# Three small broadcasts in a four-layer convolution network: from TensorE products to a round trip through memory

## The chip, the cores and the metric

The kernel runs on one core of a Trainium2 chip, in float32 throughout. The metric is the device time of one execution in microseconds. A core has TensorE (PE, with its weight loads listed apart as PEld), VectorE (DVE), ScalarE (ACT), GpSimd (POOL) and SyncE (SP), which here only issues DMAs. Each engine works through its own instructions in order.

## The reference

The input is x of shape (8, 384, 32, 32). Four layers follow one another; each adds f(GroupNorm(x)) to x. Layer 0 is an attention with depthwise convolutions ahead of it. The change concerns layers 1 and 3, and their order beside layer 2.

```
# layer 1: mixture of 4 experts, two of them kept for each token (h, w)
scores = softmax(x_flat @ gate_w + gate_b);  top_v, top_i = top_k(scores, 2)
top_w  = softmax(top_v)                       # two weights a token, their sum is 1
coef[e] = sum over k of present[k, e] * top_w[k]
out = sum over e of (w2[e] @ relu(w1[e] @ x + b1[e]) + b2[e]) * coef[e]

# layer 2: depthwise 3x3 with ternary weights, then a pointwise product

# layer 3: deformable attention, 3 groups of 128 channels
q   = q_w @ x
off = gelu(batchnorm(depthwise 5x5, stride 2, of q))         # 16 x 16 points a group
om  = pw_w @ off                                             # 3 rows: y, x, modulation
offset, modulation = om[0:2], sigmoid(om[2:3])
pos = tanh(offset) * (1/16) * 2 + reference points
x_s = bilinear samples of x at pos, times sigmoid(modulation)
k, v = kv_w @ x_s;  out = proj_w @ attention(q, k, v) + proj_b
```

## The kernel before, in words

Channels lie on the 128 partitions, in KC = 3 chunks; an image has N = 1024 pixels, and HALF is 512. Layer 0 takes the first half of the time and is not touched. What follows is one pass over the eight images.

**Layer 1** of an image is a list of 48 units (`layer1`, from L1184). For each half of the pixels there are 12 hidden units (`hidden`, L1260: three matmuls of 128 x 512, a Relu on ScalarE, and in `weight` a product with the token's coefficient on VectorE, L1246), and then 12 result units (`result`, L1281: three matmuls each; four units make one 128-channel output, which VectorE adds to x at L1287). `enter` forms the unit's input. In between stand two small steps for each half:

- `spread(h)` (L1219 to L1228) brings the tokens' first weight w0 to all partitions. `route` leaves w0 as [128 tokens, 8 images x 8 blocks]. Four matmuls (L1224) take a column of it, repeated 128 times, as the stationary operand and the identity as the moving one; VectorE copies the PSUM bank into the tile w0s (L1228), which has one buffer.
- `bias(h)` (L1233) and `weight` (L1242, on ScalarE) read w0s.

The first image is run in another way (`late=True`): its hidden units are done while the routing is still open.

**Layers 2 and 3** of an image are generators. Layer 2 takes statistics (L103), normalises (L144), does the nine taps on VectorE (L1347, L1355), then the pointwise product (`pw`, L1363), and stores x through SP (L1371). Layer 3 makes q (L1400), transposes the image into xT (L1423), does 25 taps for the offsets on VectorE (L1470) and a Gelu (L1475). Then it makes `om`: for each of three rows r, the weights of the row, repeated over 128 columns (`pw3[:, r, :]`), are multiplied with the 768 points in two matmuls (L1483, L1484), so that the row's result stands on all 128 partitions; ScalarE's Tanh (L1487) brings it from PSUM into the tile om{r}. From gy and gx (rows 0 and 1; L1493, L1497) come "tents", relu(1 - |position - pixel|), on ScalarE (L1501, L1502, L1515, L1516), multiplied on GpSimd (L1517); from row 2 comes md (L1498, L1499). Eight blocks of pixels are sampled by matmuls of xT with the tents (L1521, tiles xsb and xs), and VectorE multiplies with md (L1528). Keys and values (L1535, L1544), the attention (L1561 to L1614) and the last product (`pf`, L1666) follow.

**The order.** In the main loop image b's layers 2 and 3 run beside image b+1's layer 1. The generator yields numbers, the microseconds in which TensorE is held to have nothing of this image to do; they are added up in `due`, and whenever `due` reaches UNIT = 2.6, one unit of layer 1 is issued. What is left of the 48 units is issued after the generator has ended. The yields of one image are:

| part of the image | yields, us |
|---|---|
| layer 2 up to the end of the taps | 43.3 |
| layer 3 up to the Gelu and the break (`yield None`) | 44.85 |
| the three om rows | 3 x 0.3 |
| the elementwise work on om | 6.0 |
| the first sampled block's tents; the eight blocks | 2.0; 8 x 0.5 |
| up to the end of the attention | 17.5 |

At b = 6 the remaining units are all issued at the break; what follows of image 6 runs beside image 7's layers 2 and 3. When the program is built, an instruction may be put ahead of others of its engine that are not ready: in the trace the next image's entry (L1211) runs ahead of this image's last product. The tiles of tag "flat" (five buffers of 4 KB a partition) are shared by loads of layer 0's output, the offsets, the tents and the attention's probabilities. PSUM has two tiles of two banks ("big"), three banks for layer 1 (`fbank`) and one more (`vbank`).

**Queues.** Almost all DMAs are issued by SP, in order: the stores of x after layer 2 (L1371), the next image's loads (`load_image` L169, which waits for xT's buffer, and L1195, which waits for flat buffers), and the output (L1677).

```
offf = off.rearrange("p g h w -> p (g h w)")
nc.scalar.activation(offf, offf, AF.Gelu, bias=bo3, scale=so3)
yield 3.0
yield None
...
while due >= UNIT and units:
    units.pop(0)()
    due -= UNIT
```

Of the kernel before, what the change touches and what calls it, by code (L numbers as in the profile page):

```python
# [7 lines left out]
F32 = mybir.dt.float32  # L8
AF = mybir.ActivationFunctionType
# [3 lines left out]
B, C, H, W = 8, 384, 32, 32  # L13
N = H * W
P = 128
KC = C // P
HALF = N // 2
# [15 lines left out]
NPAIR3, HS, LS, NG = 3, 16, 256, 3  # L33
# [19 lines left out]
def tile_kernel(ctx: ExitStack, tc: tile.TileContext, i: dict, out: bass.AP):  # L53
    nc = tc.nc
# [4 lines left out]
    dram = ctx.enter_context(tc.tile_pool(name="dram", bufs=1, space=bass.MemoryType.DRAM))  # L59
# [157 lines left out]
    with ExitStack() as pa:  # L217
# [10 lines left out]
        for s in range(2):  # L228
            t = wa.tile([P, KC, H + 2, W], F32, name=f"pad{s}")
# [124 lines left out]
        with tc.issue_after(stacked[0].ins):  # L354
            load_x(1)
            nc.sync.dma_start(out=cw[:, 3:], in_=i["cw"][:, 3:])
            ident = load_const("ident")
# [6 lines left out]
        for n, (b, g) in enumerate(work):  # L364
# [6 lines left out]
            if n in todo:  # L371
                f, b2 = todo.pop(n)
# [10 lines left out]
            for h, k in steps:  # L383
                dx, c0, c1, o0 = TAPS[k]
                rows = slice(h * (H // 2), (h + 1) * (H // 2))
                if g < NGC:
                    lhs, rhs = cw[:, g, dx, :], st[:, rows, c0:c1]
                else:
                    r = slice(32 * h, 32 * h + 3 * GR)
# [550 lines left out]
    def load_w(name):  # L940
        src = i[name]
        t = wd.tile(list(src.shape), F32, tag=name, name=name + "_sb")
        nc.sync.dma_start(out=t, in_=src)
        return t
# [8 lines left out]
    def fbank(name):  # L953
        return ps_f.tile([P, HALF], F32, tag="f", name=name)
# [17 lines left out]
    pl = Pools(pd, "d")  # L972
    w1, b1 = load_w("w1"), load_w("b1")
    w0 = wd.tile([P, B, NT8], F32, name="w0")
    pres = wd.tile([P, 2, NE], F32, name="pres")
    nc.vector.memset(pres, 0.0)
    gws = wd.tile([P, NE], F32, name="gws")
# [58 lines left out]
    def route(units, end):  # L1036


        ls = pl.one([P, HALF], "ts", "ls")
        nc.vector.tensor_copy(ls, plog)  # L1040

        pt = fbank("plt").rearrange("p (q a b e) -> p q a b e", q=8, a=2, b=B)
        for q in range(4):
            nc.tensor.matmul(
                pt[:, q].rearrange("p a b e -> p (a b e)"), lhsT=ls[:, q * P : (q + 1) * P],
                rhs=sel2, start=True, stop=True,
            )
        nc.tensor.matmul(
            pt[:, 4, 0].rearrange("p b e -> p (b e)"), lhsT=ones,
            rhs=tb.rearrange("p b e -> p (b e)"), start=True, stop=True,  # L1050
        )
        gb = wd.tile([P, B, NE], F32, name="gb")
        nc.vector.tensor_tensor(
            gb, pt[:, 4, 0], gbias.unsqueeze(1).to_broadcast([P, B, NE]), ALU.add
        )
        nt = B * NT8
        lg = pl.one([P, B, NT8, NE], "vt", "lg")
        for a in range(2):
            for q in range(4):
                nc.vector.tensor_tensor(lg[:, :, 4 * a + q, :], pt[:, q, a], gb, ALU.add)  # L1060
        l = lg.rearrange("p b t e -> p (b t) e")
        wk = pl.one([P, 3, nt, NE], "kt", "routing")
        wv = pl.one([P, 5, nt], "om2", "routed")

        def bc(ap):
            return ap.unsqueeze(2).to_broadcast([P, nt, NE])

        sc, eq, oh = (wk[:, k] for k in range(3))
        m = wv[:, 4]
        nc.vector.reduce_max(m, l, AX.X)  # L1070
        nc.vector.tensor_tensor(l, l, bc(m), ALU.subtract)
        nc.scalar.activation(sc, l, AF.Exp)
        nc.vector.reduce_sum(m, sc, AX.X)
        nc.vector.reciprocal(m, m)
        nc.vector.tensor_tensor(sc, sc, bc(m), ALU.mult)
        tops = []
        for k in range(2):
            mk, ek = wv[:, 2 * k], wv[:, 2 * k + 1]
            nc.vector.reduce_max(mk, sc, AX.X)

            nc.vector.tensor_tensor(eq, sc, bc(mk), ALU.is_equal)
            nc.vector.tensor_tensor(
                eq, eq, ewt.unsqueeze(1).to_broadcast([P, nt, NE]), ALU.mult
            )
            nc.vector.reduce_max(ek, eq, AX.X)
            nc.vector.tensor_tensor(oh, eq, bc(ek), ALU.is_equal)
            nc.vector.reduce_max(pres[:, k, :], oh.rearrange("p t e -> p e t"), AX.X)
            if k == 0:
                nc.vector.scalar_tensor_tensor(sc, oh, -2.0, sc, ALU.mult, ALU.add)
            tops.append(mk)  # L1090
        while len(units) > end:
            units.pop(0)()
        pp_ = fbank("ppres")
        nc.tensor.matmul(
            pp_[:, : 2 * NE], lhsT=ones, rhs=pres.rearrange("p k e -> p (k e)"),
            start=True, stop=True,
        )
        nc.vector.tensor_scalar(
            prs.rearrange("p k e -> p (k e)"), pp_[:, : 2 * NE], 0.0, None, ALU.is_gt
        )  # L1100
        nc.vector.tensor_tensor(m, tops[1], tops[0], ALU.subtract)
        nc.scalar.activation(m, m, AF.Exp)
        nc.vector.tensor_scalar(m, m, 1.0, None, ALU.add)
        nc.vector.reciprocal(w0.rearrange("p b t -> p (b t)"), m)

    prs = wd.tile([P, 2, NE], F32, name="prs")
    dp = wd.tile([P, NE], F32, name="dp")
# [55 lines left out]


    x2_dram = dram.tile([B, P, KC, N], F32, name="x2")
    NU3 = 2 * NPAIR3
    rec3 = wd.tile([P, B * NU3, 16], F32, name="rec3")
    bad3 = wd.tile([P, 1], mybir.dt.int32, name="bad3")
# [15 lines left out]
    def layer1(pl, b, late=False):  # L1184
# [33 lines left out]

        def spread(h):  # L1219

            pw = fbank(f"w0_{b}_{h}")
            for t in range(4):
                wt = w0[:, b, 4 * h + t : 4 * h + t + 1].to_broadcast([P, P])
                nc.tensor.matmul(  # L1224
                    pw[:, t * P : (t + 1) * P], lhsT=wt, rhs=ident, start=True, stop=True
                )
            state["w0", h] = pl.one([P, HALF], "w0", f"w0s{b}_{h}")
            nc.vector.tensor_copy(state["w0", h], pw)  # L1228
# [64 lines left out]
        def unit(*calls):  # L1293
            units.append(lambda: [f(*a) for f, *a in calls])

        if late:
            for h in range(2):
                unit((enter, h), (hidden, h, 0))
                for k in range(1, NE * KC):
                    unit((hidden, h, k))  # L1300
            for h in range(2):
                for m in range(KC):
                    for part in range(4):

                        w, n = (0, part) if h == m == 0 else (1, 4 * m + part - 4)
                        first = []
                        if n == 0:
                            first += [(spread, w), (bias, w)]
                        if h == 0 and n < 4:
                            first += [(weight, w, 3 * n + k) for k in range(3)]  # L1310
                        unit(*first, (result, h, m, part))
            return units
        for h in range(2):
            if h == 0:
                unit((enter, 0), (spread, 0), (bias, 0), (hidden, 0, 0))
            else:
                unit((bias, 1), (hidden, 1, 0))
            for k in range(1, NE * KC):
                unit((hidden, h, k))
            for m in range(KC):  # L1320
                for part in range(4):
                    if h == 0 and m == 2 and part == 0:
                        unit((result, h, m, part), (enter, 1), (spread, 1))
                    else:
                        unit((result, h, m, part))
# [48 lines left out]
    def layer3(pl, b, xt, put, general):  # L1374
# [103 lines left out]
        yield None  # L1478

        om = []  # L1480
        for r in range(3):
            po = big(f"pom_{b}_{r}")
            nc.tensor.matmul(po[:, :512], lhsT=pw3[:, r, :], rhs=offf[:, :512], start=True, stop=True)  # L1483
            nc.tensor.matmul(po[:, 512:768], lhsT=pw3[:, r, :], rhs=offf[:, 512:], start=True, stop=True)  # L1484
            t = pl.one([P, NG * LS], f"om{r}", f"om{r}_{b}")

            nc.scalar.activation(t, po[:, : NG * LS], AF.Tanh, scale=1.0 if r < 2 else 0.5)  # L1487
            om.append(t)
            yield 0.3
# [195 lines left out]
    for b in range(1, B):  # L1685
        logits(b)
        del fetched[b, 0]
        for n in (2, 3) if b == 1 else (b + 2,):
            if n < B:
                fetch_next(n)  # L1690
        if b + 3 == B:
            w2, b2 = load_w("w2"), load_w("b2")
            wq3, wk3, wv3, wp3 = (load_w(n) for n in ("wq3", "wk3", "wv3", "wp3"))
            pb3, dw3, bn3, pw3 = (load_w(n) for n in ("pb3", "dw3", "bn3", "pw3"))
            ref3, npos = load_w("ref3"), load_w("npos")
        if b + 1 < B:
            for _ in range(3 if b < 6 else 2):
                units.pop(0)()
# [81 lines left out]
def _layouts(a):  # L1780
# [3 lines left out]
    L = {}  # L1784
# [49 lines left out]
    for n in "qk":  # L1834
# [27 lines left out]
    L["bn3"] = np.stack(  # L1862
        [a[f"L3_conv_{n}"] for n in ("dw_b", "bn_w", "bn_b", "bn_mean", "bn_var")], axis=1
    )
    L["pw3"] = np.repeat(a["L3_conv_pw_w"].T[:, :, None], P, axis=2)
    lin = np.linspace(0.5, HS - 0.5, HS, dtype=f) / f(HS) * f(2.0) - f(1.0)
    ref = np.stack([np.repeat(lin, HS), np.tile(lin, HS)])
# [26 lines left out]
```

## Time and profile before

| what | value |
|---|---|
| median of 3 runs | 3751.69 us (3746.74 to 3756.45) |
| the profiled execution | 3751.05 us, its span 3749.3 us |
| mean granted TensorE clock | 0.981 |
| HBM read, written | 122.64 MB, 75.50 MB |
| layer 1's result and hidden matmuls (L1281, L1260) | 490.2 and 483.3 us of PE |
| layer 2's taps (L1355) | 234.0 us of DVE |
| layer 3's taps (L1470) | 213.1 us of DVE |

A float32 matmul stands in the trace as two records; "x6" is three matmuls. In a timeline a row gives start, duration, engine, line, operation, written tile <- read tiles, sizes and count, and in brackets the idle time ahead of it with what ended it. In the waits view a row gives who waited for whom, the total, the number of times, and the longest.

### The profile page before, as it was taken

The numbers are of one execution on the slowest core, as the hardware profiler recorded it, in microseconds if no ns is written. First come the engines' busy times: TensorE is split into PE (matmuls) and PEld (weight loads), VectorE is DVE, ScalarE is ACT, GpSimd is POOL, SyncE is SP. The second block draws the span as 40 slices with busy tenths as digits, with TensorE's granted clock in tenths as the row PEclk, the third lists the DMA queues.
The fourth block names the chain that finished last, engine by engine and source line by source line (L and its number), as shares of the span: only waits on it lengthen the run. The fifth ranks groups of instructions, "written<-read, shape, count | busy, mean of one in ns | idle before, by whom it ended". The sixth has DMA issues, their size and how long they took to land.

```text
span 3749.3 us, 39325 instructions
## 1 busy us (share of the span) xinstructions
PE 3632.0 (97%) x15746; PEld 1533.0 (41%) x15746; DVE 1820.6 (49%) x2840; ACT 1280.2 (34%) x1536; POOL 199.5 (5%) x162
## 2 busy tenths in 40 slices
PE   7999999999999999999799999999999999999888
PEld 3444333333333333333244534444444444544433
DVE  6776223232323232333346557465663656547664
ACT  2222354545444454534112321323222232322222
POOL 0000100000000000000000010201001010010111
PEclk8999999999999999999899999999999999999898
DMA  6776311121212121211430000100001001010000
GB/s 198 232 251 229 131 54 36 62 63 37 63 40 75 26 72 28 71 43 55 183 140 34 17 34 17 40 28 17 34 17 51 17 17 40 19 43 17 0 34 18
DMA packets 83449, 242.49 MB, mean 65 GB/s; under 512 B 18563, under 2 KB 19091, under 8 KB 82873
## 3 DMA queue, kind: packets, MB, share of 16 engines
q1 hardware_dynamic: 70174, 200.42, 16.1%
q10 hardware_dynamic: 12504, 37.88, 3.0%
q8 instruction: 128, 2.10, 0.2%
q0 software_dynamic: 576, 1.55, 0.1%
q14 instruction: 67, 0.54, 0.0%
HBM read 122.64 MB, written 75.50 MB: 53 GB/s over the span
## 4 chain that ended last, share of the span: by engine, by line
PE 40%; DVE 9%; ACT 1%; issue 0%; DMA 0%; POOL 0%; DVEq 0%; POOLq 0%; ACTq 0%; SPq 0%
PE y L1281 11%; PE ph L1260 8%; DVE y L1355 6%; PE pq L1400 3%; PE pw L1363 3%; PE pf L1666 3%; PE s L1561 3%; PE pav L1577 2%; PE pss L1603 1%; DVE hd L1246 1%; DVE off L1470 1%; PE pk L1535 1%; PE pv L1544 1%; PE xsb L1521 1%; PE pom L1483 1%; PE plog L1023 0%
## 5 line engine op out<-in xcount | busy, mean ns | idle before, releaser
L645 ACT ACTIVATE p<-s 128x1024 f32<-128x1024 f32 x512 | 496.5, 1021 | 506.8 <-PE s L638 506.6
L1281 PE MATMUL y<-hd,w_sb 128*128 128x512 f32 x1080 | 490.2, 599 | 3.6 <-DVE hd L1246 3.6
L653 PE MATMUL pav<-p,vt 64*64 64x512 f32 x4096 | 487.0, 590 | 0.0
L1260 PE MATMUL ph<-h,w_sb 128*128 128x512 f32 x1104 | 483.3, 594 | 0.4 <-DMA w_sb<-in_w_dram 0.4
L638 PE MATMUL s<-qk,qk 48*64 48x512 f32 x3072 | 370.8, 597 | 3.3 <-ACT p L645 3.3
L391 PE MATMUL pk<-st,cw_sb 126*126 126x512 f32 x720 | 322.8, 610 | 9.5 <-DMA st<-pad 9.3
L1260 PEld LDWEIGHTS ph<-h,w_sb 128*128 128x128 f32 x1104 | 207.6, 190 | 253.5 <-issue 250.3
L1281 PEld LDWEIGHTS y<-hd,w_sb 128*128 128x128 f32 x1080 | 199.0, 191 | 249.3 <-issue 235.5
L653 PEld LDWEIGHTS pav<-p,vt 64*64 64x64 f32 x4096 | 156.6, 133 | 285.1 <-issue 285.1
L610 DVE COPY ta<-pav 128x512 f32<-128x512 f32 x64 | 44.2, 691 | 429.0 <-PE pav L653 425.9
L1355 DVE SCALAR_TENSOR_TENSOR y<-h,tap,y 128x992 f32<-128x992 f32 (+1 forms) x192 | 234.0, 1242 | 1.6
L391 PEld LDWEIGHTS pk<-st,cw_sb 126*126 126x126 f32 x720 | 140.4, 197 | 183.8 <-issue 179.1
L1470 DVE SCALAR_TENSOR_TENSOR off<-q,dw_sb,off 128x225 f32<-128x225 f32 (+3 forms) x432 | 213.1, 546 | 1.7
L1270 ACT ACTIVATE hd<-ph,b_sb 128x512 f32<-128x512 f32 x180 | 122.7, 681 | 258.6 <-PE ph L1260 258.3
L638 PEld LDWEIGHTS s<-qk,qk 48*64 48x64 f32 x3072 | 108.6, 133 | 231.1 <-issue 191.9
L78 DVE COPY qk<-pq 128x512 f32<-128x512 f32 x48 | 33.2, 691 | 292.7 <-PE pq L572 292.7
L397 ACT COPY y<-pk 126x512 f32<-126x512 f32 (+1 forms) x136 | 76.4, 583 | 255.2 <-PE pk L391 111.1
L1568 ACT ACTIVATE p<-s 128x1024 f32<-128x1024 f32 x96 | 93.1, 1021 | 173.0 <-PE s L1561 172.9
L590 PE MATMUL po<-att,wo_sb 128*128 128x512 f32 x288 | 132.8, 615 | 11.6 <-DMA att<-al 11.6
L1246 DVE TENSOR_TENSOR hd<-hd,cb 128x512 f32<-128x512 f32 x180 | 122.3, 684 | 35.5 <-ACT hd L1270 35.2
L1363 PE MATMUL pw<-y,upw 128*128 128x512 f32 x288 | 129.7, 603 | 7.6 <-DVE y L1355 7.6
L572 PE MATMUL pq<-g,wq_sb 128*128 128x512 f32 x288 | 131.2, 606 | 2.2 <-DMA wq_sb<-in_wq_dram 2.2
(280 smaller groups left out, 3961.2 us busy)
## 6 DMA issues: line engine op xcount, KB each, us to landing
g<-raw SPq DMA_DIRECT2D x72, 512.0 KB
st<-pad SPq DMA_DIRECT2D x180, 168.0 KB
raw<-y ACTq DMA_DIRECT2D x171, 168.0 KB
xa<-in_x_dram SPq DMA_DIRECT2D x24, 512.0 KB
xh<-in_x_dram SPq DMA_DIRECT2D x48, 256.0 KB
f<-in_x_dram SPq DMA_DIRECT2D x24, 512.0 KB
f<-o SPq DMA_DIRECT2D x24, 512.0 KB
o<-ot SPq DMA_DIRECT2D x42, 256.0 KB
```

What stands on the lines that cost most here:

```text
L391: nc.tensor.matmul(pk[h].rearrange("p (h w) -> p h w", w=W)[: 3 * nch, :, o0 : o0 + c1 - c0], lhsT=lhs, rhs=rhs, start=(k == 0), stop=(k = ...
L572: nc.tensor.matmul(pq, lhsT=w_in[v][:, c, pr * P : (pr + 1) * P], rhs=acts[b][v][:, c, h * HALF : (h + 1) * HALF], start=(c == 0), stop=(c ...
L590: nc.tensor.matmul(po, lhsT=wo0[:, c, m * P : (m + 1) * P], rhs=atts[b][:, c, hs], start=(c == 0), stop=(c == KC - 1),)
L638: nc.tensor.matmul(s[64 * k : 64 * k + 64, j * HALF : (j + 1) * HALF], lhsT=kt[r, k0 : k0 + 64], rhs=qt[r, h * HALF : (h + 1) * HALF], sta ...
L645: nc.scalar.activation(p, s, AF.Exp, scale=scale)
L653: nc.tensor.matmul(pav[k][64 * j : 64 * j + 64, :], lhsT=vts[b % 2][r, kc, 2 * hd : 2 * hd + 2, :].rearrange("p a b -> p (a b)"), rhs=p[r, ...
L1246: nc.vector.tensor_tensor(hd, hd, state["cb"], ALU.mult)
L1260: nc.tensor.matmul(ph, lhsT=w1[:, e, c, dc * P : (dc + 1) * P], rhs=state["h1"][c], start=(c == 0), stop=(c == KC - 1),)
L1281: nc.tensor.matmul(y, lhsT=w2[:, e, dc, m * P : (m + 1) * P], rhs=state[h, k], start=(k == 0), stop=(k == NE * KC - 1),)
L1355: nc.vector.scalar_tensor_tensor(d, f, tap2[:, c, t : t + 1], d, ALU.mult, ALU.add)
L1363: nc.tensor.matmul(pw[h], lhsT=upw2[:, c, m * P : (m + 1) * P], rhs=y[c][:, hs], start=(c == 0), stop=(c == KC - 1),)
L1470: nc.vector.scalar_tensor_tensor(d, f, dw3[:, t : t + 1], d, ALU.mult, ALU.add)
```

## The change

1. **Tokens' weights.** At the end of `route` the tile w0 is transposed on TensorE, copied by VectorE, and stored to a DRAM tile w0_dram of [8, 1024] by SP. In `spread` (all images but the first) one DMA issued by SP reads the 512 values of the half for every partition into w0s. `spread(0)` is called when the image's units are made, right after its loads, not in the first unit; `spread(1)` stays where it was.
2. **Offsets and modulation.** For images 0 to 5 one product with the three weight columns gives the three rows on three partitions (two matmuls, 512 and 256 columns). One Tanh, with each partition's own scale from the new constant half3 (1, 1, 0.5), writes them into a flat tile; one DMA stores them to om_dram, and three DMAs each read one row for every partition into om0, om1 and om2. A yield of 7.0 takes the place of three of 0.3. Images 6 and 7 and the recomputation path keep the three products.
3. The constant half3 is loaded with the others.

```
     pl = Pools(pd, "d")
     w1, b1 = load_w("w1"), load_w("b1")
     w0 = wd.tile([P, B, NT8], F32, name="w0")
+    w0_dram = dram.tile([B, N], F32, name="w0d")
...
-        nc.vector.reciprocal(w0.rearrange("p b t -> p (b t)"), m)
+        w0f = w0.rearrange("p b t -> p (b t)")
+        nc.vector.reciprocal(w0f, m)
+
+        wt = fbank("w0t")
+        nc.tensor.transpose(wt[:nt, :P], w0f, ident)
+        wr = pl.one([P, HALF], "ts", "w0r")
+        nc.vector.tensor_copy(wr[:nt, :P], wt[:nt, :P])
+        nc.sync.dma_start(out=w0_dram.rearrange("b (t p) -> (b t) p", p=P), in_=wr[:nt, :P])
...
     x2_dram = dram.tile([B, P, KC, N], F32, name="x2")
+    om_dram = dram.tile([B, 3, NG * LS], F32, name="omd")
...
         def spread(h):
 
+            if not late:
+                ws = state["w0", h] = pl.one([P, HALF], "w0", f"w0s{b}_{h}")
+                hs = slice(h * HALF, (h + 1) * HALF)
+                nc.sync.dma_start(out=ws, in_=w0_dram[b : b + 1, hs].to_broadcast([P, HALF]))
+                return
             pw = fbank(f"w0_{b}_{h}")
...
+        spread(0)
         for h in range(2):
             if h == 0:
-                unit((enter, 0), (spread, 0), (bias, 0), (hidden, 0, 0))
+                unit((enter, 0), (bias, 0), (hidden, 0, 0))
...
         om = []
-        for r in range(3):
+        if b < B - 2:
+
+            po = big(f"pom_{b}")
+            for k in (slice(0, 512), slice(512, 768)):
+                nc.tensor.matmul(po[:3, k], lhsT=pw3[:, :, 0], rhs=offf[:, k], start=True, stop=True)
+            t = pl.flat([P, NG * LS], f"oms_{b}")
+            nc.scalar.activation(t[:3], po[:3, : NG * LS], AF.Tanh, scale=half3)
+            nc.sync.dma_start(out=om_dram[b], in_=t[:3])
+            for r in range(3):
+                t = pl.one([P, NG * LS], f"om{r}", f"om{r}_{b}")
+                nc.sync.dma_start(out=t, in_=om_dram[b, r : r + 1].to_broadcast([P, NG * LS]))
+                om.append(t)
+            yield 7.0
+        for r in range(0 if om else 3):
             po = big(f"pom_{b}_{r}")
...
+    L["half3"] = np.array([[1.0], [1.0], [0.5]], f)
```

More of the change, by code (lines that the diff above doesn't have):

```diff
@@ L1694, in tile_kernel @@
             pb3, dw3, bn3, pw3 = (load_w(n) for n in ("pb3", "dw3", "bn3", "pw3"))
-            ref3, npos = load_w("ref3"), load_w("npos")
+            ref3, npos, half3 = load_w("ref3"), load_w("npos"), load_w("half3")
         if b + 1 < B:
```

## The prediction, made before the changed kernel was run

> **What bounds the kernel now.** I read the page first: shares of the engines, then busy time by stage, then TensorE's own order in one image, then its waits.
>
> ```profile
> PE 3632.0 (97%) x15746; PEld 1533.0 (41%) x15746; DVE 1820.6 (49%) x2840; ACT 1280.2 (34%) x1536; POOL 199.5 (5%) x162
> ```
> ```profile
> 2003.00:2231.00 228.00, 226.67 (x658) 102.49 (x657) 135.00 (x200) 63.87 (x88) 20.54 (x17) 1.00 0.08 28
> 2231.00:2458.00 227.00, 225.50 (x654) 101.90 (x653) 135.41 (x198) 62.30 (x85) 20.02 (x16) 1.00 0.08 28
> ```
> The second fence is busy time in windows (columns: window, length, busy PE, PEld, DVE, ACT, POOL, granted clock, DMA share, GB/s): two of the six image periods in which image b's layers 2 and 3 run beside image b+1's layer 1. PE is busy in all but about 1.4 of 228 us, at full clock, and the DMA engines are nearly idle. An instruction taken from PE there is worth its whole duration, if nothing new makes PE wait. What makes it wait now, in the waits view from 2003 to 3500:
>
> ```profile
> PE pw L1363 <- DVE y L1355: 4.7, 7, 0.7
> PE pav L1577 <- ACT p L1568: 3.3, 6, 0.5
> ```
> So once an image, for 0.7 us, the pointwise product waits for VectorE's depthwise convolution: in that stretch VectorE is the bound by a hair. PE's order around the products that the change touches (timeline, image 0: start, us):
>
> ```profile
> 2120.78 1.02 PE L1483 MATMUL pom<-off,pw_sb 128*128 128x512 f32 x2
> 2121.64 0.59 PE L1484 MATMUL pom<-off,pw_sb 128*128 128x256 f32 x2
> 2122.07 1.02 PE L1483 MATMUL pom<-off,pw_sb 128*128 128x512 f32 x2
> ...
> 2124.65 5.31 PE L1260 MATMUL ph<-h,w_sb 128*128 128x512 f32 x12
> 2129.80 2.74 PE L1281 MATMUL y<-hd,w_sb 128*128 128x512 f32 x6
> 2132.37 0.54 PE L1521 MATMUL xsb<-wt,xT 128*128 128x48 f32 x4
> ...
> 2215.48 7.89 PE L1281 MATMUL y<-hd,w_sb 128*128 128x512 f32 x18
> 2223.20 1.05 PE L1224 MATMUL w<-ident_sb,w 128*128 128x128 f32 x8
> 2224.09 2.74 PE L1260 MATMUL ph<-h,w_sb 128*128 128x512 f32 x6
> ```
> One om product lasts 2122.07-2120.78 = 1.29 us from start to start, one spread 2224.09-2223.20 = 0.89, one unit of layer 1 (six records) 5.15/2 = 2.58. Between the om products and the sampling (L1521) three units keep PE busy.
>
> **What the skill says.** "TensorE: Matmul & The Clock Gate", Step-by-step, has a matmul's time set by the columns streamed, not by the width of the result. The trace agrees as far as it goes (0.86 us for 512 columns, 0.43 for 256); so one product with 3 result rows should cost what one with 128 costs. "ScalarE: Activation LUTs", Step-by-step, gives one element per cycle and lane: a Tanh on 3 partitions costs what it costs on 128, 0.81 us here. "DMA: Bandwidth & Descriptors", Anatomy of one DMA, gives some 2.0 us fixed for each DMA, mostly the receipt of the write; its Rules for kernel authors want a read of freshly written memory to wait for the writer's semaphore. So store and reads come one after the other. Loads in this trace fit:
>
> ```profile
> 2186.15 7.03 SPq L1195 DMA_DIRECT2D o<-o  x3
> 2196.40 1.28 DVE L1211 SCALAR_TENSOR_TENSOR x<-o,bnsc_out,x 128x1024 f32<-128x1024 f32 x1 [0.50 <-DMA o<-o]
> 2141.00:2148.00 7.00, 7.00 (x27) 4.94 (x26) 1.31 (x3) 0.00 (x0) 0.00 (x0) 1.00 0.66 228
> ```
> The last 512 KB load is issued about 2192.9 and frees VectorE at 2196.40: 3.5 us. The three loads of the same size in the last row's window (issued 2140.48) ran at 228 GB/s with the engines 0.66 busy, so at 228/0.66 = 345 GB/s while busy: 512 KB is 1.5 us of data, and 2.0 us are fixed.
>
> **The change, part by part.**
>
> Taken from PE: the spreads of images 1 to 7, 14 x 0.89 = 12.5 us; two of three om products of images 0 to 5, 12 x 1.29 = 15.5. Sum 27.9. Images 6 and 7 keep three om products, and image 0 its spreads. On other engines 14 copies of 0.68 us (VectorE) and 12 Tanhs of 0.81 (ScalarE) go; only the copies lie on a path (below).
>
> Added once, in the routing: a transpose (two records of 0.28 us), a short VectorE copy, a 32 KB store. The weights are ready at 1921.96 and the first spread starts at 1925.71, behind the presence product at 1925.57, so the transpose fits among hidden units; I add 0.3 us to the path. Uncovered, the store would delay image 1's load behind it on SP; its reader comes 70 us later.
>
> Spread by DMA, 14 times 256 KB: 2.0 + 0.8 = 2.8 us. The first half's stands behind the image's loads on SP, the last issued at 2192.9, so it lands by about 2197; VectorE first needs it at 2224.80: 27 us of cover. For image 1 the cover is 1 to 2 us (loads done 1995.7, use 1998.3). The second half's comes after the layer-2 stores (last about 2056.5), four units before its use: covered. If late, it would block VectorE in front of the statistics for the convolution; nothing suggests it.
>
> The om trip is the new wait. After the one product: Tanh 0.81 + 0.1 handover; store of 9 KB, 2.0 by the page's price (no row here shows a small store; I keep 1.5 to 3.5); three reads of 384 KB, 1.18 MB / 345 = 3.4, plus 2.0 fixed = 5.4 (to 7.2 at 228 GB/s). The last plane lands 8.3 us after the product. SP holds up nothing with this wait: the next image's loads behind it wait for the sampling (issued 2140.48) now too. Then, as now, from the end of md's Tanh (2125.81) to the end of the first tent product on GpSimd (2129.31): 3.5 us. ScalarE and VectorE wait in order, behind them only later work of this step and evacuations of units that come after. The three rows also take one of the five flat buffers that the tents use, but only until their store has landed, before the first tent. The sampling can start 11.8 us after the product.
>
> Its cover is the moved units. With 88.15 us of yields before the break, 33 units are out and 2.35 us are left over. 7.0 brings three units, of which one runs ahead of the product while it waits for the Gelu, as now; 6.0 brings two, 2.0 one: five after the product, 5 x 2.58 = 12.9 us. 12.9 against 11.8: no stall in the middle case. I allow 0.3 us an image for tents that no longer run ahead (eight at 0.8 us on ScalarE, 0.67 us each on PE): 6 x 0.3 = 1.8.
>
> The units come from the end. Yields sum to 118.55 now, 45 of 48 units, and three remain after the last product (y x18 at 2215.48); with 6.1 more, 47 are out and one remains. That costs nothing: the convolution's path starts when the last unit ends, and the units between that and its product stay 16.
>
> That path, 2223.4 to 2269.1, loses a 0.67 us copy while PE's cover loses 0.89: the wait of 0.7 grows by 0.22. The offset convolution is similar (Gelu done 2120.0, product 2120.78). 7 x 0.22 = 1.5; none if the bias steps (2.0 us) start earlier with the earlier weights, and then up to 7 x 0.7 = 4.9 gained; at worst 14 x 0.22 = 3.1.
>
> Sum: 27.9 - 0.3 - 1.8 - 1.5 = 24.3. The profiled execution took 3751.05 us (span 3749.3), 0.6 below the median: 3751.05 - 24.3 = 3726.8; I say 3727.
>
> **The rivals.**
>
> *The trip outlasts its cover a little.* Store 3.5, reads 7.2: 0.9 + 3.5 + 7.2 + 3.5 = 15.1, 2.2 over 12.9; 6 x 2.2 = 13, so 3740. For it: only 1.1 us of slack. Against: the DMA engines are idle just then.
>
> *Reading one row 128 times is slow.* No row shows such a read. At a quarter of the loads' rate the data take 13.6: the last plane at 18.5, sampling at 22.0, 9.1 us of stall in each of six images: 3751.05 - 24.3 + 55 = 3782, slower. It decides from a stall of about 4.3 us an image (24.3/6 = 4.05 beyond the allowance of 0.3), the last plane later than 13.7. Against: descriptors stay 3 KB long and go to 128 partitions, much like the loads.
>
> *The saving is given back.* The three-row product, other unit positions in the attention part, or VectorE's two tight stretches take 20 us back: 3747. For it: both stretches are tight within 0.7 us. Against: each loses a copy too.
>
> **Numbers.** Forecast 0.70 (3718 to 3733), short overrun 0.15 (3733 to 3745), given back 0.09, slow reads 0.06. A measurement here tells 0.3%, 11 us, from no change. Faster by more: 0.70 + 0.09 of the overrun = 0.79; slower: 0.06; same: 0.15. The range 3718 to 3742 holds the forecast and most of the overrun.
>
> **What would show it.** Right: PE's image period falls by some 4.1 us (2.57 + 1.78 less small waits); no idle before L1521; six y records, not 18, after the last layer-3 product; no VectorE wait on the w0 load. Wrong: idle before the sampling released by GpSimd or the om loads, a growing wait of pw on the convolution, or a three-row product unlike 1.29 us.

## The result, and the profile after

| what | before | after |
|---|---|---|
| median, four runs each on one chip | 3753.86 us (3746.74 to 3756.45) | 3719.14 us (3716.66 to 3720.45) |
| the profiled execution, its span | 3751.05, 3749.3 us | 3716.66, 3714.9 us |
| from image 0's q product (L1400 of before) to image 6's: six image periods | 1363.9 us | 1331.8 us |

The ratio is 0.991 (95% interval 0.9896 to 0.9923): the changed kernel is faster, by 34.7 us by medians, where 24.3 were forecast. The sign and the mechanism held; the size did not hold as well, for 3719.14 lies only 1.1 us inside the fast end of the stated range. The extra comes from places that the sum did not have, and the experiments below look for them.

The page's shares of the engines, after (instructions behind the x):

```profile
PE 3598.4 (97%) x15587; PEld 1504.2 (40%) x15587; DVE 1810.6 (49%) x2827; ACT 1273.6 (34%) x1524; POOL 195.9 (5%) x162
```

TensorE is as full as it was, with less to do: 33.6 us less of busy time. Two image periods after (window, length, busy PE, PEld, DVE, ACT, POOL, granted clock, DMA share, GB/s):

```profile
1997.00:2219.00 222.00, 221.15 (x634) 98.04 (x634) 133.10 (x197) 62.25 (x84) 19.53 (x16) 1.00 0.11 37
2219.00:2441.00 222.00, 221.00 (x632) 97.70 (x631) 134.24 (x198) 61.45 (x83) 19.55 (x16) 1.00 0.11 37
```

A period is 222.2 us now (1331.8/6), 5.3 less than before; the forecast said some 4.1. PE lacks 0.9 us in it, where it lacked 1.4. The DMA engines rise from 28 to 37 GB/s: the new traffic, still a tenth of their time.

TensorE's own order around the product, image 0 of after (start, duration, line, operands, records):

```profile
2113.34 1.46 PE L1500 MATMUL pom<-off,pw_sb 128*3 128x512 f32 x4
2114.73 7.99 PE L1274 MATMUL ph<-h,w_sb 128*128 128x512 f32 x18
2122.56 7.89 PE L1295 MATMUL y<-hd,w_sb 128*128 128x512 f32 x18
2130.28 0.54 PE L1549 MATMUL xsb<-wt,xT 128*128 128x48 f32 x4
...
2212.53 2.74 PE L1295 MATMUL y<-hd,w_sb 128*128 128x512 f32 x6
2215.11 2.74 PE L1274 MATMUL ph<-h,w_sb 128*128 128x512 f32 x6
```

Read from above: one product instead of three; then six units of layer 1, 15.55 us; then the sampling (L1549), with no bracket of idle time ahead of it. At the end of the image six records of y remain instead of 18, and no spread stands between them and the hidden units. The round trip itself, on SP, and its use on VectorE and GpSimd (SPq is SP's queue; the start is the issue):

```profile
2109.33 0.33 SPq L1233 DMA_DIRECT2D w0s<-w0d  x1
...
2115.75 0.26 SPq L1503 DMA_DIRECT2D omd<-oms  x1
2117.31 1.27 SPq L1506 DMA_DIRECT2D om<-omd  x3
...
2140.92 2.52 SPq L169 DMA_DIRECT2D x<-in_x_dram  x3
```
```profile
2121.51 0.95 DVE L1521 SCALAR_TENSOR_TENSOR om<-om,ref_sb 128x768 f32<-128x768 f32 x1
...
2127.36 2.70 POOL L1545 TENSOR_TENSOR wt<-wt,om 128x144 f32<-128x144 f32 x5 [70.82 <-ACT om L1530]
...
2196.18 0.74 DVE L1247 SCALAR_TENSOR_TENSOR x<-w0s,yb,x 128x512 f32<-128x512 f32 x1
...
2250.75 0.74 DVE L1247 SCALAR_TENSOR_TENSOR x<-w0s,yb,x 128x512 f32<-128x512 f32 x1
```

The store goes out at 2115.75, and SP issues the reads that wait for it at 2117.31, 1.56 us later; the trace has the last plane landed at 2123.03. The next image's load behind them is issued at 2140.92 and waits for the sampling, as before (2140.48, in an image that began 4 us later): SP's wait for the store holds up nothing. The first weight half is asked for at 2109.33, ahead of all this. L1247 are the bias steps.

The waits of PE from 1997 to 3480 (waiter, line <- whom; total, times, longest):

```profile
PE pav L1605 <- ACT p L1596: 3.3, 6, 0.5
PE pw L1378 <- DVE y L1370: 2.0, 7, 0.3
```

No wait of the sampling is among them, and that on the convolution has shrunk from 4.7 to 2.0 us. So where did the time go? Sums from start to start of PE's groups over the six periods (changes from the unrounded sums):

| group | before | after | change |
|---|---|---|---|
| spreads (w) | 10.7 | 0 | -10.7 |
| om products (pom) | 23.2 | 8.3 | -14.9 |
| scores of layer 3 (s) | 88.9 | 82.6 | -6.3 |
| pointwise products with their waits (pw) | 98.3 | 96.1 | -2.1 |
| layer 1's units (y, ph) | 756.2 | 758.5 | +2.3 |
| rest | | | -0.3 |
| six periods | 1363.9 | 1331.8 | -32.0 |

Outside them: layer 0 ends 4.4 us earlier (the presence product starts at 1921.2 instead of 1925.6), though no instruction there is changed. The routing up to image 0's q product takes 0.3 us more, and image 6's second part with image 7 takes 1.7 more. -32.0 - 4.4 + 0.3 + 1.7 = -34.4, the difference of the spans.

The surprise is the scores: 288 records in both kernels, none of them touched by the diff.

### The profile page after: what moved, and what is told of

Same layout as the page of the kernel before. It is cut to its first block, busy times and chain, and to the rows that moved or that the text cites. A ratio compares the mean times of both kernels' runs of the same rounds, so it can differ in the third digit from the quotient of the medians.

```text
span 3714.9 us, 39037 instructions
## 1 busy us (share of the span) xinstructions
PE 3598.4 (97%) x15587; PEld 1504.2 (40%) x15587; DVE 1810.6 (49%) x2827; ACT 1273.6 (34%) x1524; POOL 195.9 (5%) x162
## 4 chain that ended last, share of the span: by engine, by line
PE 39%; DVE 10%; ACT 1%; issue 1%; DMA 0%; POOL 0%; DVEq 0%; ACTq 0%; POOLq 0%; SPq 0%
PE y L1295 11%; PE ph L1274 8%; DVE y L1370 6%; PE pq L1415 3%; PE pf L1694 3%; PE pw L1378 3%; PE s L1589 3%; PE pav L1605 2%; DVE hd L1260 1%; PE pss L1631 1%; PE pk L1563 1%; PE pv L1572 1%; DVE off L1485 1%; PE xsb L1549 1%; PE px L1438 1%
## 5 line engine op out<-in xcount | busy, mean ns | idle before, releaser
L391 PE MATMUL pk<-st,cw_sb 126*126 126x512 f32 x720 | 320.3, 606 | 12.7 <-DMA st<-pad 10.9
L1370 DVE SCALAR_TENSOR_TENSOR y<-h,tap,y 128x961 f32<-128x961 f32 (+1 forms) x192 | 234.1, 1244 | 0.6
```

Of the source, the lines that this page charges most:

```text
L391: nc.tensor.matmul(pk[h].rearrange("p (h w) -> p h w", w=W)[: 3 * nch, :, o0 : o0 + c1 - c0], lhsT=lhs, rhs=rhs, start=(k == 0), stop=(k = ...
L1370: nc.vector.scalar_tensor_tensor(d, f, tap2[:, c, t : t + 1], d, ALU.mult, ALU.add)
```

## The experiments

The number given is the difference of medians to the kernel before on the same chip, with the ratio's interval. Beside it stands the length of the six periods in the trace, which leaves layer 0 out. Where a run is set beside the changed kernel, the two medians come from different comparisons, in which the kernel before took 3750.49 to 3753.86; such a distance can be some 3 us off, and the six periods weigh more. Each program keeps the rest of the kernel it starts from.

**The weights' part alone** (the changed kernel, three om products everywhere):

```
-        if b < B - 2:
+        if b < 0:
```


> Only the tokens' weights go through memory; all images keep three om products and the old yields. Theory (PE's removed instructions count in full, and the bias steps that now run during the last product shorten the convolution's path): 14 x 0.89 = 12.5 us for the spreads and about 2 us of the wait of pw on the convolution, so some 14 us below the kernel before. Rival (VectorE sets the tight stretches, so a spread is worth only its 0.67 us copy): 14 x 0.67 = 9.4 us below.

Measured: 3736.52 against 3750.49, -14.0 (0.9971, 0.9961 to 0.9980). The six periods are 13.3 shorter: w -10.7, pw -2.2, and the scores unchanged at 88.9. PE's wait on the convolution is 1.9 us in all. So the part gives its 12.5 us of spreads, and about 2 us of waits on top, where the prediction had reckoned a loss of 1.5 (3.1 at worst).

**The offsets' part alone** (the changed kernel with the old spreads):

```
-            if not late:
+            if False:
...
-        spread(0)
...
-                unit((enter, 0), (bias, 0), (hidden, 0, 0))
+                unit((enter, 0), (spread, 0), (bias, 0), (hidden, 0, 0))
```
(the routing's transpose, copy and store are taken out too)

> Only the offsets and modulation go through memory, with the yield of 7.0; the tokens' weights are spread by products as before. Theory (trip covered, and one split pair of score matmuls fewer in each of six images): 12 x 1.29 = 15.5 and 6 x 1.04 = 6.2, so some 21 us below the kernel before. Rival (only the products count): 15.5 below. Rival (the trip shows): less than 15.

Measured: 3730.55, -19.9 (0.9953, 0.9939 to 0.9966). The six periods are 19.0 shorter: pom -14.9, s -6.3, pw -0.1, the rest +2.3. The two parts together give 14.0 + 19.9 = 33.9: they add up to the whole change, and the gain in the scores belongs to this part, that in pw to the other.

**The yields alone.** The kernel before, with the total of the new yields and nothing else. A yield says only how many units are issued there:

```
-            yield 0.3
+            yield 0.3 if r < 2 or b >= B - 2 else 6.4
```


> The kernel before with one number changed: the last of the three om yields is 6.4, not 0.3, for images 0 to 5; no product and no DMA is changed. The order built has two split pairs of score matmuls an image, not three, and one unit after the last product, not three. Theory (a split pair costs 1.04 us): 6.2 us below the kernel before. Rival (where the units stand is of no account; the extra gain has another cause): within 2 us of it.

Measured: 3746.88 over 13 runs, -3.6 (0.9992, 0.9984 to 1.0001). By time alone it is inconclusive, since the interval holds no change. The trace is not: the six periods are 5.2 shorter, s -6.3 and y +1.5. The line that shows it, in the six periods, for the kernel before and then for this one (busy us, mean ns | idle):

```profile
L1561 PE MATMUL s<-q,kt 64*128 64x512 f32 x288 | 91.6, 622 | 0.0
```
```profile
L1561 PE MATMUL s<-q,kt 64*128 64x512 f32 x288 | 84.9, 619 | 0.0
```

The mean of one record is nearly the same, the number is the same, and the busy time, which counts overlapping records once, is 6.7 us smaller. So it is not the instruction that became faster; it is how much of them lies beside one another.

**The old yields in the changed kernel**, the counterpart:

```
-            yield 7.0
+            yield 0.9
```


> The changed kernel with the yield of 7.0 put back to 0.9, the sum of the old three. The order built still has five units between the om product and the sampling, but three split pairs an image. Theory (the order is filled at build time whatever the yield says, so the trip stays covered but for some 0.2 us; the pairs cost 6 x 1.04): about 7 us above the changed kernel. Rival (the yield is what covers the trip): three units instead of six, a stall of some 5 us in six images, about 30 us above the changed kernel.

Measured: 3723.90, -26.6 (0.9937, 0.9924 to 0.9951), 4.8 above the changed kernel. Its six periods are 6.0 longer, all of it in the scores (+6.3). Before the sampling it has:

```profile
2117.27 7.99 PE L1274 MATMUL ph<-h,w_sb 128*128 128x512 f32 x18
2125.10 5.31 PE L1295 MATMUL y<-hd,w_sb 128*128 128x512 f32 x12
2130.47 0.65 PE L1549 MATMUL xsb<-wt,xT 128*128 128x48 f32 x4
```

Five units stand between product and sampling without the long yield, 13.2 us, where the yields alone would have put three, and the sampling waits for less than 0.1 us. The rival's 30 us of stalls failed: the order as built fills the trip with units that are ready. The 7.0 adds a sixth, but it earned its place elsewhere, by shifting the units in the attention.

**Why the scores are shorter.** One call of `scores` is four matmuls of 512 columns (eight records), alternately on the lower and the upper 64 partitions. The Trainium skill, "TensorE: Matmul & The Clock Gate", Part 3 (The mechanism), says that matmuls on different row groups of the array overlap. The trace of before agrees (image 0):

```profile
2158.82 1.99 PE L1561 MATMUL s<-q,kt 64*128 64x512 f32 x8
2160.74 1.08 PE L1603 MATMUL pss<-p,ones 128*64 128x512 f32 x4
2161.75 1.12 PE L1561 MATMUL s<-q,kt 64*128 64x512 f32 x2
2162.80 1.94 PE L1577 MATMUL pav<-p,vt 128*64 128x512 f32 x8
2164.67 1.98 PE L1561 MATMUL s<-q,kt 64*128 64x512 f32 x6
```

Together the four take 2160.74 - 2158.82 = 1.92 us. When one of them is put ahead of pav, it takes 2162.80 - 2161.75 = 1.05 alone, and the other three still take 1.91 (from start to start in the image's third split, 2186.01 to 2187.92): 2.96, so a split costs 1.04 us. In each of the six images, before has three splits and after two: 6 x 1.04 = 6.2, against 6.3 measured. That reading called for a direct test: keep the four together, in both kernels. The new argument pins the matmuls of all calls but the first to their place in the program.

```
-        def scores(pr, h):
+        def scores(pr, h, pin=False):
...
-                    nc.tensor.matmul(
+                    mm = nc.tensor.matmul(
...
+                    if pin:
+                        tc.keep_in_program_order(mm)
...
-                    ps = scores(*units[u + 1])
+                    ps = scores(*units[u + 1], True)
```
**In the changed kernel:**

> The changed kernel with the four score matmuls of a unit pinned behind the attention product ahead of them, so that the built order has no split pair in any image (two in each of images 0 to 5, one in image 6 and five in image 7 now). Theory (a split pair costs 1.04 us of PE): 12 x 1.04 = 12.5 us below the changed kernel, up to 19 with the last two images, less what PE then waits for the exponentials. Rival (the pairs are of no account): within 2 us of it or slower for the lost freedom.

Measured: 3712.53 against 3751.73, -39.2 (0.9897, 0.9882 to 0.9912), 6.6 below the changed kernel. The scores of the six periods, 84.9 us after, are here:

```profile
L1589 PE MATMUL s<-q,kt 64*128 64x512 f32 x288 | 71.5, 615 | 0.0
```

and no split in its order:

```profile
2166.18 1.99 PE L1589 MATMUL s<-q,kt 64*128 64x512 f32 x8
2168.09 1.08 PE L1633 MATMUL pss<-p,ones 128*64 128x512 f32 x4
2169.10 1.12 PE L1295 MATMUL y<-hd,w_sb 128*128 128x512 f32 x2
2170.16 1.94 PE L1607 MATMUL pav<-p,vt 128*64 128x512 f32 x8
```

The mechanism holds, its size was over-reckoned: start to start the scores give 10.9 us, but the six periods gain 8.5. Where a score matmul filled the time before pav, a y matmul fills it now, and the y group is 2.4 us longer. Images 6 and 7 gave nothing (their part 321.0 against 321.4): there pav waits 7.2 us for VectorE (`ts`), which it did not do before the pin.

**In the kernel before:**

> The kernel before with the same pin on the score matmuls and nothing else. Theory: 18 x 1.04 = 18.7 us below the kernel before, up to 25 with images 6 and 7, less new waits. Rival: within 2 us of it. Beside the run of the changed kernel with pairs kept, it also tells what the change is worth when the pairs play no part: theory 28 us and about 2 of the convolution's wait.

Measured: 3736.54, -15.2 (0.9964, 0.9952 to 0.9976); six periods -15.4, of it s -18.9 and y +3.5. Without the splits on either side, the change is worth 3736.54 - 3712.53 = 24.0 us by medians and 1348.5 - 1323.3 = 25.2 in the six periods. That takes most of the surprise away: what the prediction summed up is there at about the size it gave in all, and the splits came on top. Single terms were off and in part made up for each other (below).

**What frees the convolution.** My first reading was that the wait of pw shrank because `spread(0)` is called early. So it goes back into the first unit, as a DMA:

```
-        spread(0)
...
-                unit((enter, 0), (bias, 0), (hidden, 0, 0))
+                unit((enter, 0), (spread, 0), (bias, 0), (hidden, 0, 0))
```


> The changed kernel with the first half's weights fetched in the image's first unit, where the spread stood before, not when the units are made. Theory (the early fetch lets the bias steps run during the last product and takes 2 us of VectorE off the convolution's path): the wait of pw on the convolution returns, 2 to 5 us above the changed kernel, unless the fetch is built early anyway. Rival (early or late is the same): within 1 us.

Measured: 3720.64, -31.1 (0.9920, 0.9907 to 0.9934); six periods 1331.8, those of the changed kernel. The theory fell in this form. The fetch is built early anyhow, and the bias steps with it; SP and VectorE of this run:

```profile
2112.18 0.33 SPq L1233 DMA_DIRECT2D w0s<-w0d  x1
```
```profile
2198.77 0.74 DVE L1247 SCALAR_TENSOR_TENSOR x<-w0s,yb,x 128x512 f32<-128x512 f32 x1
```

In the kernel before, the same three steps stood in front of the convolution, behind the last y, as they needed PE's product:

```profile
2225.61 2.04 DVE L1233 SCALAR_TENSOR_TENSOR x<-w0s,yb,x 128x512 f32<-128x512 f32 x3
```

So it is the fetch itself that lets them run some 25 us earlier in the image (counted from its q product), during the attention, and not the line on which it is called.

What that gives shows from the image's last unit, as its result reaches VectorE, to the first tap of the next convolution, before and then after:

```profile
2223.40 0.75 DVE L1287 SCALAR_TENSOR_TENSOR x<-y,yb,x 128x512 f32<-128x512 f32 x1 [6.44 <-PE y L1281]
...
2232.07 0.75 DVE L1347 TENSOR_SCALAR y<-h,tap 128x1024 f32<-128x1024 f32 x1 [0.71 <-ACT h L144]
```
```profile
2215.31 0.75 DVE L1301 SCALAR_TENSOR_TENSOR x<-y,yb,x 128x512 f32<-128x512 f32 x1 [1.29 <-PE y L1295]
...
2221.49 0.75 DVE L1362 TENSOR_SCALAR y<-h,tap 128x1024 f32<-128x1024 f32 x1 [1.31 <-ACT h L144]
```

8.67 us became 6.18, in each of images 1 to 6. Before, the copy of the weights (0.67) and the three bias steps (2.04) stood on VectorE among the steps of the statistics that the convolution needs; now they do not.

**The reads taken twice.** Does the trip have room, and are the broadcast reads dear?

```
-                nc.sync.dma_start(out=t, in_=om_dram[b, r : r + 1].to_broadcast([P, NG * LS]))
+                for _ in range(2):
+                    nc.sync.dma_start(out=t, in_=om_dram[b, r : r + 1].to_broadcast([P, NG * LS]))
```


> The changed kernel with the three rows read twice, the second pass over the first, so that the trip is longer by a pass of reads, some 4 us. Theory (the trip lies beside units of layer 1, and more units are put there at build time): within 3 us of the changed kernel; what stall there is shows ahead of the sampling. Rival (the trip is on the path): 6 x 4 = 24 us above it.

Measured: 3718.91, -32.8 (0.9911, 0.9898 to 0.9925), the time of the changed kernel; six periods +0.3. Between product and sampling stand now 38 records of units instead of 36:

```profile
2116.97 7.99 PE L1274 MATMUL ph<-h,w_sb 128*128 128x512 f32 x18
2124.80 8.75 PE L1295 MATMUL y<-hd,w_sb 128*128 128x512 f32 x20
2133.38 0.54 PE L1550 MATMUL xsb<-wt,xT 128*128 128x48 f32 x4
```

The trip did become longer: the first tent product is ready at 2132.70, 15.7 us after the product's end, not 13.1. It costs nothing, since PE has units to take, and the sampling starts 16.4 us after the product. The rival of the slow reads, 3782 in the prediction, is out.

**All eight images.** Images 6 and 7 have few or no units beside their products. What does the trip cost without cover?

```
-        if b < B - 2:
+        if b < B:
```


> The changed kernel with the offsets' trip through memory for images 6 and 7 too, where no units of layer 1 are left to cover it. Theory (a trip that nothing covers costs its length: 13 us from the product to the sampling, against 2.6 us of further products and some 8 us of idle PE now): PE's idle time ahead of the sampling of these two grows from 12.3 to some 20 us, and the time is 3 to 8 us above the changed kernel. Rival (the trip is cheap even bare): within 2 us of it.

Measured: 3726.66 against 3751.66, -25.0 (0.9935, 0.9922 to 0.9949), 7.5 above the changed kernel. Waits of the sampling from 3393 to the end, after and then here:

```profile
PE xsb L1549 <- POOL wt L1545: 12.3, 2, 7.9
```
```profile
PE xsb L1549 <- POOL wt L1545: 24.3, 2, 12.2
```

The waits grow by 12.0 us, and the four products that are saved give 4 x 1.29 = 5.2 back: 6.8; the trace of this part is 6.4 longer, the medians 7.5 apart. So without units beside it the trip costs 6 us more of waiting for the tents an image, some 3.4 net of the two products. The cover decides the sign. Other things moved in this part too (the wait of the om product for the Gelu is 11.3 us instead of 6.7, a wait of 3.0 for the convolution is gone, and the mean granted clock is 0.89 instead of 0.91), so the size is less sure than the sign.

**The second bias step.** Most of the 2.5 us that the weights' part freed on VectorE ahead of the convolution is lost again: the second half's weights also come early (SP issues their fetch at 2234.83), and its bias steps then run at 2250.75, 2252.54 and 2254.36, in the middle of the next image's convolution, 3 x 0.74 us ahead of the pw that waits. Pinned behind the steps ahead of them:

```
-                nc.vector.scalar_tensor_tensor(
+                up = nc.vector.scalar_tensor_tensor(
...
+                if h == 1 and not late:
+                    tc.keep_in_program_order(up)
```


> The changed kernel with the three bias steps of the second half pinned behind what stands ahead of them in the program, so that they leave the convolution's stretch, into which the early fetch had let the build put them (2.2 us of VectorE an image). Theory (that stretch is the bound for PE by 0.3 us): the rest of the wait of pw on the convolution goes, some 2 us below the changed kernel. Rival (the steps then delay the offsets' taps and the Gelu instead): PE idles ahead of the om product, no gain or a loss of 1 to 6 us.

Measured: 3714.79, -36.9 (0.9902, 0.9886 to 0.9917). By medians that is 4.4 below the changed kernel, but the intervals overlap. The trace decides: the six periods are 2.6 shorter (1329.2), pw 96.1 to 93.5, and the row of pw is gone from PE's waits:

```profile
PE pav L1607 <- ACT p L1598: 3.3, 6, 0.5
PE gna_d L114 <- DVE mv_d L108: 1.0, 1, 1.0
PE ph L1276 <- ACT h L1223: 0.3, 1, 0.3
```

What follows the six periods took 1.6 us longer here than in the changed kernel's trace, at a mean granted clock of 0.90 instead of 0.91; of the four executions timed, the traced one is the slowest.

**Both pins.**

> The two pins together: score matmuls kept in pairs and the second half's bias steps kept in place. Theory (the two are independent): the gain of the pairs, 6.6 us below the changed kernel, and whatever the bias pin gives by itself, about 2 us more. Rival (both draw on the same slack of PE): no better than the pairs alone.

Measured: 3706.44, -45.2 (0.9879, 0.9864 to 0.9894), 12.7 below the changed kernel. Its six periods take 1320.7, 11.1 less than after, which is the sum of 8.5 and 2.6. It is the fastest of all programs run.

## Why the prediction was right, and where its sum was short

**TensorE's removed work, 27.9 us: held.** In the six periods lie 12 of the 14 spreads, 10.7 us, and all of the om products. They gave 14.9 instead of 15.5: the product with three rows takes 2114.73 - 2113.34 = 1.39 us, not 1.29. That the streamed columns set the time (the Trainium skill, "TensorE: Matmul & The Clock Gate", Step-by-step) was right to a tenth of a microsecond.

**The trip: most parts near their estimates, covered by luck in one place.** Product's end to last plane: 8.3 us forecast, 2123.03 - 2114.73 = 8.3 measured. The Tanh took 0.89 us instead of 0.81, the store 1.56 instead of 2.0, the reads 5.7 instead of 5.4: two misses that cancel. (The Trainium skill, "DMA: Bandwidth & Descriptors", gives the 2.0 under Anatomy of one DMA for those issued by GpSimd; these are issued by SP, and what bore the price was its fit to this trace's loads.) GpSimd's five tent products start at 2127.36 and take 2.70 us, so the first was ready at about 2127.9, 13.1 us after the product, not 11.8: the elementwise steps took 4.9 instead of 3.5. Had the cover been the 12.9 of the prediction, the sampling would have been 0.2 us late each time. It was 15.55: six units stood there, not five. The old-yield run, with five instead of the three that its yields give, shows that the number hangs on the yield only in part, since ready units are taken in any case. The "short overrun" rival failed on both sides: its prices were not reached (13.1 us to the first use, not 15.1), and the cover of 15.55 would have held even against them.

**The allowance of 1.8 us for tents that no longer run ahead: about right in its sum, not in its place.** No wait of the sampling shows in the six periods; layer 1's units are 2.3 us longer instead. Whether that is the same time in another place was not tested.

**The wait of the convolution: wrong in sign.** The forecast was 1.5 us lost. It fell by 2.7 (4.7 to 2.0 over seven images), since the bias steps no longer stand ahead of the convolution. The prediction had named that as its "up to 7 x 0.7 = 4.9 gained", if the bias steps start earlier, and did not take it. The step that failed is their place: "VectorE first needs it at 2224.80" leaves them where they stood, but they ran from 2196.18, right behind the step that completes their input (L1220, which starts at 2194.97 and takes 1.28). The fetch was misplaced as well ("behind the image's loads on SP", landing "by about 2197"; it was issued at 2109.33), but a landing at 2197 would have let them run hardly later. The program's order was taken for the built order, in the second half too: its bias steps moved into the next convolution, and the pinned run shows that this cost the rest. PE's loss of cover, 0.89, was made up: four of the pointwise matmuls stand ahead of the wait now (x8 at 2256.76), where three did (x6 at 2265.74).

**The routing, 0.3 us: net, 0.3 was measured**, but one spread (image 1's first) lies in the same stretch, so the change costs 1.2 elsewhere in it. Of that, 0.96 is one new wait of PE, for the first statistics of image 0's layer 2 (gna_d at 1995.84); before has none there, nor has the run with the offsets alone.

**What no term had: the score matmuls, 6.3 us.** "Given back" spoke of "other unit positions in the attention part" and gave them only a loss. They brought a gain: one split of an overlapping group less in each image. The two kernels without splits, 24.0 us apart by medians and 25.2 in the six periods, show that the sum of the other terms was about right. It was so by luck in part. From the forecast of 24.3 to the 34.4 of the two spans: scores +6.3, layer 0 +4.4, the wait of the convolution +3.6, rest +0.3; against them image 6's second part and image 7 -2.6 (1.7 and the spread that went there), the routing -0.9 (1.2 instead of 0.3), the om product's 1.39 and the units -0.5 each. Without the first two that is 23.7, in which the others cancel.

**And layer 0.** 4.4 us of the two profiled executions' difference lie in instructions that the change does not touch. In the window from 50 to 100 us the granted clock was 0.86 before and 0.93 after, the DMA engines moved 198 and 221 GB/s, and TensorE did 103 and 113 matmul records; by 400 us the changed kernel was 8 records ahead (857 and 865). Which of clock and loads led was not tested.

Over all 13 traces the presence product starts between 1921.2 and 1929.3. The changed kernel's profile is the earliest of them, and without layer 0 the two traces differ by 30.0 us. The kernel before took 3750.49 to 3751.73 in the three later comparisons, with more runs, against 3753.86 here. So 34.7 is likely a few us too much. The run with `spread(0)` moved back, whose order in the six periods is the same, was 31.1 us below its kernel before.

**What stays open.** Image 6's second part and image 7 take 1.7 us more (319.7 to 321.4), although a spread (0.89) has gone there. The part is 318.9 with the weights alone, 318.7 with the offsets alone (their yields included), 318.9 with both and the old yields, and 321.4 with all. So it takes weights, offsets and yields together. The mean granted clock in this part is 0.92 in the kernel before and in the three others, and 0.91 with all. Whether the clock is the cause or follows from where PE waits was not settled.

## What to carry to other kernels

Where one engine is busy in 99 of 100 us, work moved from it to idle DMA engines is worth its full duration, as long as ready work covers the trip: here 8.3 us to the last plane and 13.1 to its first use were free beside 15.6 us of units, and cost 6 us more of waiting an image where nothing lay beside them. When a step's input no longer comes from the busy engine, ask where the built order will put the step, for it may land early where it helps (bias steps in the attention) and early where it hurts (bias steps in the next convolution). And where work is shifted past groups of matmuls that overlap, count the groups that are split before and after: a split was worth 1.04 us here, and the mean duration of a record does not show it, only the group's busy time against its count.

## What was not expected of the hardware

- Four score matmuls on alternating halves of 64 partitions take 1.92 us when they are adjacent, and 2.96 when one is apart: three of them alone take 1.91, as long as all four.
- Three rows of 3 KB, each read into 128 partitions, 1.18 MB in all: 5.7 us from the first issue to the last landing, near the estimate of 5.4 made from ordinary loads. Nothing in it shows a penalty for reading one place 128 times.
- From the issue of the 9 KB store of three partitions to the issue of the reads that wait for it: 1.56 us.
- A product with three result rows lasts 1.39 us against 1.29 with 128. Its three weight columns also lie 128 apart in memory; which of the two it is was not separated. In the same way its Tanh took 0.89 us on 3 partitions, with a scale of each partition's own, against 0.81 on 128 with a fixed one.
- The granted clock early in the program differed between executions, 0.86 and 0.93 in the same 50 us, and layer 0 ended between 1921.2 and 1929.3 us over 13 executions.
